# Gate and up projections of an MLP by Strassen's seven block products, in a Mamba, MLP and expert kernel on one Trainium2 core

## The chip, the cores and the metric

The kernel runs on one core of one Trainium2 chip. A core has five engines that run side by side, each through its own list of instructions in order: TensorE (PE) multiplies matrices, VectorE (DVE), ScalarE (ACT) and GpSimd (POOL) work on vectors, SyncE (SP) issues transfers. ACT and POOL issue some transfers too.[...] Matrix products land in PSUM, a memory of eight banks per core, from which DVE and ACT take them. The metric is the device time of one execution in microseconds (us).

## What is computed

All arithmetic is in 32-bit floats. There are 2048 tokens of 512 numbers. The reference, cut to what matters:

```python
x = x + attn_ref(layernorm(x), ...)
x = x + ffn_ref(layernorm(x), ...)

def attn_ref(hidden_states, ...):
    residual = hidden_states
    h = rmsnorm(hidden_states, ln1_w)
    h = residual + mamba2(h, ...)
    residual = h
    h2 = rmsnorm(h, ln2_w)
    mlp = silu(h2 @ gate_w) * (h2 @ up_w) @ down_w
    return residual + mlp

def mamba2(x, ...):
    z, xb, Bc, Cc, dt = split(x @ in_proj_w)
    xBC = silu(causal_depthwise_conv(concat(xb, Bc, Cc)))
    dt = softplus(dt + dt_bias)
    y = ssd_chunked(x_h * dt, dt * A, B_h, C_h) + D * x_h
    return rmsnorm(y * silu(z), norm_w) @ out_proj_w
```

gate_w and up_w are 512x2048, down_w is 2048x512. ffn_ref picks 2 of 8 experts for each token and sums their weighted outputs.

## The kernel before

The code is one function written in a tile language: the program says which tiles exist, how many buffers a kind of tile has, and in which engine an operation runs. A scheduler then puts the instructions of each engine in an order, by the program's order and its own idea of when things are ready. So instructions of different stages come to stand between each other.

Four stages run over the tokens.

- Mamba, in blocks of 256 tokens (`mamba`, L650 on). `prepare` normalizes x and turns it (`hn`, `pt`, `hT`), and computes dt with many small DVE steps (`pdt`, L214 to L236). `project` multiplies by in_proj (`pm`, L300), ACT copies the result out (`pre`, L310), DVE runs the convolution as eight steps a pair (L317 and L319), ACT applies Silu (L323). `gate` makes z (`pz`, L300, Silu L329). `chunk` runs the state-space part for 128 tokens: 16 Exps on ACT (L367), products with dt on DVE (L369), matmuls `psc`, `py`, `pst`. At its end ACT squares y, POOL adds the squares up (`sq`, L427), PE sums them over partitions (`pms`, L430), and PE multiplies y by out_proj (`po`, L437). `pms` is written ahead of `po`.
- MLP, in blocks of 512 tokens (`feed_forward`, `mlp`, `mlp_down`). For each chunk c of 128 of the 2048 hidden columns: `pg` and `pu` are four matmuls each of a 128x128 weight block with 512 columns of h2T; ACT takes Silu of pg (L594), DVE multiplies by pu (L595). For every two chunks, `mlp_down` makes four products `pd` (L603) that DVE adds to the rows (L606). There are 4 blocks x 16 chunks. The first three blocks run in between the Mamba steps, one chunk per step; the fourth runs after Mamba, while expert weights are loaded.
- Routing (`route`), for each block of 512 tokens, in between the next block's chunks.
- Experts (`tiles`), 39 tiles of 128 gathered tokens, after the MLP.

PSUM before: a ring of two banks for transposes and small sums (`ps_tr`), a ring of three for pm, pz, po, pg, pu and pd (`ps_mm`), one tile of two banks for psc, one bank for py. For the last MLP block and the experts there are two banks each of four kinds.

SP issues nearly all loads: x, the weights of in_proj (`wi`, four buffers of 512 KB, loaded three ahead), gate, up and down weights for each chunk (`mg`, `mu`, `md`), the broadcast rows of dt sums (`cum`, `ec`). Each load waits in SP's list until its buffer is free. At the start POOL scales out_proj's weights by norm_w (L457).

The matmuls of 32-bit floats are each two instructions in the trace.

Of the kernel before, what the change touches and what calls it, by code (L numbers as in the profile page):

```python
# [15 lines left out]
P = 128  # L16
T = 2048
D = 512
# [10 lines left out]
DFF = 2048  # L29
FC = 128  # L30
# [18 lines left out]
def mamba_mlp_moe(ctx, tc, x, w_in, w_out, w_gate, w_up, w_down, par, wr, wg, wu, wd, out):  # L49
# [20 lines left out]
    xp = pa_stack.enter_context(tc.tile_pool(name="xp", bufs=6))  # L70
# [8 lines left out]
    params = const.tile([P, NPAR], F32, name="params")  # L79
# [4 lines left out]
    for t in range(NCH):  # L84
        load_x(t)
# [4 lines left out]
    def load_w_in(pair):  # L90

        w = pw.tile([P, NK, 2 * P], F32, name="wi", tag="wi", bufs=4)
        nc.sync.dma_start(out=w, in_=w_in_k[:, :, pair * 2 * P : (pair + 1) * 2 * P])
        return w

    ahead = [load_w_in(pair) for pair in range(3)]
    for t in range(NCH, 2 * NCH):
        load_x(t)
# [12 lines left out]
    late = const.tile([P, P], F32, name="late")  # L111
# [9 lines left out]
    halo = const.tile([P, 12, 3], F32, name="halo")  # L121
# [11 lines left out]
    )  # L133
    a_neg = const.tile([P, NH], F32, name="a_neg")
    nc.scalar.activation(a_neg, params[:, C_AL : C_AL + NH], AF.Exp)
    nc.vector.tensor_scalar_mul(a_neg, a_neg, -1.0)
# [26 lines left out]
    ps_tr = psa_stack.enter_context(tc.tile_pool(name="ps_tr", bufs=2, space=PSUM))  # L163
# [4 lines left out]
    use = {"g": (ps_mm, "mm"), "u": (ps_mm, "mm"), "d": (ps_mm, "mm"), "tr": (ps_tr, "tr")}  # L168
# [5 lines left out]

    def scales(b):
        lo, hi = b * NCH, (b + 1) * NCH
        for t in range(lo, hi):
            stats(wa, res[t], mv[:, t, :])
        rsqrt_eps(rstd[:, lo:hi], mv[:, lo:hi, 1])
        ms = wa.tile([P, NCH], F32, name=f"ms{lo}", tag="ms")  # L180
        nc.vector.tensor_tensor(ms, mv[:, lo:hi, 1], rstd[:, lo:hi], ALU.mult)
        nc.vector.tensor_tensor(ms, ms, rstd[:, lo:hi], ALU.mult)
        rsqrt_eps(rboth[:, lo:hi], ms)
        nc.vector.tensor_tensor(rboth[:, lo:hi], rboth[:, lo:hi], rstd[:, lo:hi], ALU.mult)
# [11 lines left out]
    def prepare(b):  # L196
# [11 lines left out]
        yield hT  # L208


        pdt = ps_tr.tile([P, NCH, NH], F32, name=f"pdt{b}", tag="tr")
# [26 lines left out]
        yield  # L238

# [4 lines left out]
        pc = ps_tr.tile([P, P], F32, name=f"pc{b}", tag="tr")  # L244
# [7 lines left out]
        pn = ps_tr.tile([P, NCH, NH], F32, name=f"pn{b}", tag="tr")  # L252
# [7 lines left out]
        psum = ps_tr.tile([P, 2, NCH, NH], F32, name=f"psum{b}", tag="tr")  # L260
# [33 lines left out]
    def projected(b, pair, pm, hT):  # L294
        w = ahead.pop(0)
        if b < NB - 1 or pair < 7:
            ahead.append(load_w_in((pair + 3) % 10))
        for m in range(2):
            for k in range(NK):
                nc.tensor.matmul(  # L300
                    pm[:, m, :], w[:, k, m * P : (m + 1) * P], hT[:, k, :], start=(k == 0), stop=(k == NK - 1)
                )

    def project(b, pair, hT, xb, cs):
# [8 lines left out]
        for m in range(2):  # L313
# [4 lines left out]
            for k in range(1, 4):  # L318
                nc.vector.scalar_tensor_tensor(  # L319
                    ca, pre[:, m, k : k + TB], cw[:, k : k + 1], ca, ALU.mult, ALU.add  # L320
                )
            dst = xb[:, ct, :] if ct < 4 else cs[(ct - 4) // 4][:, ct % 4, :]
# [8 lines left out]
    def channels(b):  # L331
        xb = wa.tile([P, 4, TB], F32, name=f"xb{b}", tag="xb")
        return xb, [wa.tile([P, 4, TB], F32, name=f"cs{b}_{g}", tag="cs", bufs=4) for g in range(2)]

    state = None
    h2T = [None] * NFB

    def chunk(b, j, dt, ncum, dtdec, cd, cum, ec, xb, cs, zs):
        nonlocal state
# [3 lines left out]
        sdt = sdiag[t % 2]  # L343


        pt = ps_tr.tile([P, 4, P], F32, name=f"ptx{t}", tag="tr")
# [5 lines left out]
        y = wa.tile([P, 8, P], F32, name=f"y{t}", tag="y")  # L352
        for gp in range(2):
# [38 lines left out]
            if gp == 0 and t < NT - 1:  # L392
                pst = ps_tr.tile([P, 2, 4, HD], F32, name=f"pst{t}", tag="tr")
# [3 lines left out]

            for i in range(4):
                at = C_D + 4 * gp + i
                nc.vector.scalar_tensor_tensor(  # L400
                    y[:, 4 * gp + i, :], xb[:, gp, tok], params[:, at : at + 1], py[:, i, :], ALU.mult, ALU.add
                )
            yg = y[:, 4 * gp : 4 * gp + 4, :]
            nc.vector.tensor_tensor(yg, yg, zs[:, 4 * gp : 4 * gp + 4, tok], ALU.mult)

        if t < NT - 1:
            new = wa.tile([P, 2, 4, HD], F32, name=f"state{t}", tag="state")
            flat = new.rearrange("p g i d -> p (g i) d")
            if t:
                nc.gpsimd.tensor_tensor(  # L410
                    flat, state.rearrange("p g i d -> p (g i) d"),
                    bc(cd[:, j].rearrange("p g i -> p (g i)"), 2, HD), ALU.mult,
                )
                nc.vector.tensor_tensor(new, new, pst, ALU.add)
            else:
                nc.vector.tensor_copy(new, pst)
            state = new
# [11 lines left out]
        pms = ps_tr.tile([P, 1], F32, name=f"pms{t}", tag="tr")  # L429
        nc.tensor.matmul(pms, sq[:, 0, :], ones[:, 0:1], start=True, stop=True)  # L430

# [3 lines left out]
        po = ps_mm.tile([P, D], F32, name=f"po{t}", tag="mm")  # L435
        for m in range(8):
            nc.tensor.matmul(po, y[:, m, :], w_o[:, m, :], start=(m == 0), stop=(m == 7))  # L437
# [14 lines left out]
        if off == 0:  # L452
            h2T[fb] = wk.tile([P, NK, FB], F32, name=f"h2T{fb}", tag="h2T")
        transposed(h2, h2T[fb][:, :, off : off + P], params[:, C_L2 : C_L2 + NK])
# [5 lines left out]
    def load_mlp(c):  # L460
        g = pmlp.tile([P, NK, FC], F32, name="mg", tag="mg")
        u = pmlp.tile([P, NK, FC], F32, name="mu", tag="mu")
        d = pmlp.tile([P, D], F32, name="md", tag="md", bufs=4)
        cols = slice(c * FC, (c + 1) * FC)
        nc.sync.dma_start(out=g, in_=w_gate[:, cols].rearrange("(k p) n -> p k n", p=P))
        nc.sync.dma_start(out=u, in_=w_up[:, cols].rearrange("(k p) n -> p k n", p=P))
        nc.sync.dma_start(out=d, in_=w_down[cols, :])
        return g, u, d

    def row(name):  # L470
        if more_rows:
            return more_rows.tile([P, D], F32, name=name, tag="row3", bufs=5)
        return wk.tile([P, D], F32, name=name, tag="row", bufs=5)

    def mid(shape, name):
        return wk.tile([P, *shape], F32, name=name, tag="mid", bufs=5)
# [109 lines left out]
    def mlp(fb, hT, c, w):  # L586
        g, u, d = w
        pg = bank("g", [FB], f"pg{fb}_{c}")
        pu = bank("u", [FB], f"pu{fb}_{c}")
        for wt, ps in ((g, pg), (u, pu)):  # L590
            for k in range(NK):
                nc.tensor.matmul(ps, wt[:, k, :], hT[:, k, :], start=(k == 0), stop=(k == NK - 1))  # L592
        a = wk.tile([P, FB], F32, name=f"a{fb}_{c}", tag="mid", bufs=5)
        nc.scalar.activation(a, pg, AF.Silu)  # L594
        nc.vector.tensor_tensor(a, a, pu, ALU.mult)  # L595
        return a

    def mlp_down(fb, rows, c, held):

        for j in range(NJ):  # L600
            pd = bank("d", [D], f"pd{fb}_{c}_{j}")
            for m, (a, d) in enumerate(held):
                nc.tensor.matmul(  # L603
                    pd, a[:, j * P : (j + 1) * P], d, start=(m == 0), stop=(m == len(held) - 1)
                )
            nc.vector.tensor_tensor(rows[j], rows[j], pd, ALU.add)  # L606

    def feed_forward(fb):

        nonlocal mlp_w, newest  # L610
        if fb == 0:
            mlp_w = load_mlp(0)
        rows = []
        held = []
        for c in range(NFC):
            w = mlp_w
            if fb < NFB - 1 or c < NFC - 1:
                mlp_w = load_mlp((c + 1) % NFC)
# [335 lines left out]
```

## Time and profile before

| | |
|---|---|
| median of 3 runs | 1628.93 us (1628.45 to 1629.21) |
| the profiled execution | 1629.27 us, of which the span in the profile is 1627.2 us |
| granted clock of PE | 0.993 of full speed |
| pd, down products (L603), busy | 225.4 us in 512 instructions |
| pm and pz, in_proj (L300), busy | 182.9 and 115.1 us in 768 and 512 instructions |
| po, out_proj (L437) | 118.4 us in 256 instructions |
| expert products (L817, L838) | 118.2, 117.8 and 107.6 us |
| first chunk's Silu of pg (L594) starts | 222.3 us |
| last one starts | 1276.8 us |

The page of a profile gives busy time by engine, then the span in 40 equal slices, each with a digit for the busy tenths; then the chain of work that ended last; then groups of instructions by line: engine, operation, tile written and tiles read, shape, count, then busy time and the mean of one in ns, then how long the engine stood idle just before them and what ended that. In the timeline each line has a start, a length, an engine, a line and an operation, and in brackets the idle time ahead of it. Busy time of a group leaves out what overlaps with other instructions of the engine, the mean does not.

### The profile page before, as it was taken

Reading aid. Unit: us, or ns where it says so; the run is one execution under the profiler, and the core shown is the slowest. Engines: PE = TensorE matmul, PEld = TensorE weight load, DVE = VectorE, ACT = ScalarE, POOL = GpSimd, SP = SyncE. Lnnn points to the kernel's source line nnn. Section 1 sums busy time; section 2 is a strip of 40 time slices with the busy share of each in tenths; the row PEclk is TensorE's granted clock in tenths of the full one; section 3 lists DMA queues with packets and bytes.
Section 4 is the critical chain, followed back from the end, with each engine's and each line's share of the span. In section 5 each row is a group of like instructions: output and inputs, shape, how many; then the busy total and the mean of one; then the engine's idle time right before and its main releaser. Section 6 shows DMA issues by size and latency. Waiting matters only on the chain.

```text
span 1627.2 us, 16530 instructions
## 1 busy us (share of the span) xinstructions
PE 1581.5 (97%) x5515; PEld 906.4 (56%) x5515; DVE 706.1 (43%) x1835; ACT 600.2 (37%) x1033; POOL 299.8 (18%) x349
## 2 busy tenths in 40 slices
PE   6989899999999999999999999999999999999997
PEld 5656565555555655555565556444444565666653
DVE  5876654544454456445454653233432342222221
ACT  4988784334342634262435333211100121111110
POOL 4332211211021102110211020000010014333321
PEclk9999899999999999999999999999999999999999
DMA  7634333323343633342335321216676124333332
GB/s 243 196 115 137 110 117 117 117 89 109 94 119 99 184 97 116 89 119 89 106 117 163 117 90 50 61 59 215 214 228 185 59 44 86 65 66 66 67 48 33
DMA packets 165202, 182.86 MB, mean 112 GB/s; under 512 B 10432, under 2 KB 125632, under 8 KB 165120
## 3 DMA queue, kind: packets, MB, share of 16 engines
q1 hardware_dynamic: 147456, 145.10, 30.3%
q0 software_dynamic: 8736, 20.45, 7.4%
q10 hardware_dynamic: 8928, 16.26, 2.7%
q8 instruction: 46, 0.75, 0.2%
q14 instruction: 36, 0.29, 0.1%
HBM read 155.04 MB, written 26.74 MB: 112 GB/s over the span
## 4 chain that ended last, share of the span: by engine, by line
PE 90%; ACT 2%; DVE 2%; DMA 2%; issue 2%; POOL 1%; SPq 0%; POOLq 0%; ACTq 0%; DVEq 0%
PE pg L592 13%; PE pu L592 13%; PE pd L603 13%; PE pm L300 9%; PE po L437 6%; PE epd L838 6%; PE epu L817 6%; PE epg L817 6%; PE pz L300 5%; PE pt L190 2%; PE psc L361 2%; PE py L388 2%; PE py L382 2%; PE pdt L214 1%; PE pl L515 1%
## 5 line engine op out<-in xcount | busy, mean ns | idle before, releaser
L592 PE MATMUL pg<-h2T,mg 128*128 128x512 f32 x512 | 231.8, 593 | 0.0
L592 PE MATMUL pu<-h2T,mu 128*128 128x512 f32 x512 | 230.2, 592 | 0.0
L603 PE MATMUL pd<-md,a 128*128 128x512 f32 x512 | 225.4, 592 | 0.0
L300 PE MATMUL pm<-hT,wi 128*128 128x256 f32 x768 | 182.9, 390 | 0.0
L595 DVE TENSOR_TENSOR a<-a,pu 128x512 f32<-128x512 f32 x64 | 44.0, 688 | 285.4 <-PE pu L592 255.9
L603 PEld LDWEIGHTS pd<-md,a 128*128 128x128 f32 x512 | 97.1, 190 | 122.3 <-issue 120.1
L592 PEld LDWEIGHTS pu<-h2T,mu 128*128 128x128 f32 x512 | 97.2, 190 | 122.0 <-issue 118.2
L300 PEld LDWEIGHTS pm<-hT,wi 128*128 128x128 f32 x768 | 145.4, 194 | 33.8 <-issue 12.6
L592 PEld LDWEIGHTS pg<-h2T,mg 128*128 128x128 f32 x512 | 96.1, 190 | 98.6 <-issue 95.5
L606 DVE TENSOR_TENSOR r<-r,pd 128x512 f32<-128x512 f32 x128 | 88.0, 687 | 116.1 <-PE pd L603 113.1
L319 DVE SCALAR_TENSOR_TENSOR ca<-pre,params,ca 128x256 f32<-128x256 f32 x288 | 127.8, 503 | 0.6
L817 PE MATMUL epg<-ew,xgT 128*128 x312 | 118.2, 461 | 0.5 <-issue 0.5
L437 PE MATMUL po<-w_o,y 128*128 128x512 f32 x256 | 118.4, 610 | 0.0
L817 PE MATMUL epu<-ew,xgT 128*128 x312 | 117.8, 459 | 0.0
L300 PE MATMUL pz<-hT,wi 128*128 128x256 f32 x512 | 115.1, 381 | 0.0
L838 PE MATMUL epd<-ew,ehT 128*128 (+1 forms) x234 | 107.6, 594 | 0.5 <-DVE ehT L831 0.5
L300 PEld LDWEIGHTS pz<-hT,wi 128*128 128x128 f32 x512 | 95.5, 190 | 13.5 <-DMA wi<-in_w_in 0.8
L367 ACT ACTIVATE cum<-cum,ncum 128x128 f32<-128x128 f32 x256 | 85.1, 391 | 25.3 <-POOL cum L281 24.8
L594 ACT ACTIVATE a<-pg 128x512 f32<-128x512 f32 x64 | 37.7, 589 | 151.8 <-PE pg L592 148.8
L367 ACT ACT_TABLE_LOAD x65 | 83.4, 1283 | 1.6 <-issue 0.6
L844 POOL DMA_INDIRECT out<-ey,idx x39 | 61.8, 1585 | 94.2 <-DVE ey L843 78.1
L798 POOL DMA_INDIRECT xg<-xnd,idx x39 | 38.3, 981 | 211.7 <-PE pt L190 187.0
(220 smaller groups left out, 1755.8 us busy)
## 6 DMA issues: line engine op xcount, KB each, us to landing
wi<-in_w_in SPq DMA_DIRECT2D x80, 512.0 KB, 3.8
mg<-in_w_gate SPq DMA_DIRECT2D x64, 256.0 KB, 2.8
mu<-in_w_up SPq DMA_DIRECT2D x64, 256.0 KB, 2.8
md<-in_w_down SPq DMA_DIRECT2D x64, 256.0 KB, 2.8
cum<-rowsd SPq DMA_DIRECT2D x32, 512.0 KB, 4.9
ec<-rowsd SPq DMA_DIRECT2D x60, 128.0 KB, 4.2
xnd<-xn ACTq DMA_DIRECT2D x28, 256.0 KB, 4.5
ew<-in_wg SPq DMA_DIRECT2D x8, 704.0 KB, 5.8
```

Of the source, the lines that this page charges most:

```text
L300: nc.tensor.matmul(pm[:, m, :], w[:, k, m * P : (m + 1) * P], hT[:, k, :], start=(k == 0), stop=(k == NK - 1))
L319: nc.vector.scalar_tensor_tensor(ca, pre[:, m, k : k + TB], cw[:, k : k + 1], ca, ALU.mult, ALU.add)
L367: nc.scalar.activation(lt[:, half, i], lt[:, half, i], AF.Exp, bias=ncum[:, j, h : h + 1])
L437: nc.tensor.matmul(po, y[:, m, :], w_o[:, m, :], start=(m == 0), stop=(m == 7))
L592: nc.tensor.matmul(ps, wt[:, k, :], hT[:, k, :], start=(k == 0), stop=(k == NK - 1))
L595: nc.vector.tensor_tensor(a, a, pu, ALU.mult)
L603: nc.tensor.matmul(pd, a[:, j * P : (j + 1) * P], d, start=(m == 0), stop=(m == len(held) - 1))
L606: nc.vector.tensor_tensor(rows[j], rows[j], pd, ALU.add)
L798: nc.gpsimd.indirect_dma_start(out=xg, out_offset=None, in_=src, in_offset=bass.IndirectOffsetOnAxis(ap=idx[:, n : n + 1], axis=0))
L817: nc.tensor.matmul(ps, xT[:, k, :], w[:, lo : lo + EI], start=(k == 0), stop=(k == NK - 1))
L838: nc.tensor.matmul(pd, hT[:n, m, :], w[:n, NG + m * D : NG + (m + 1) * D], start=(m == 0), stop=(m == len(ET) - 1))
L844: nc.gpsimd.indirect_dma_start(out=out, out_offset=bass.IndirectOffsetOnAxis(ap=idx[:, n : n + 1], axis=0), in_=y, in_offset=None, compute ...
```

## The change

The gate and up products of a chunk are seen as one product of two by two blocks: the weights [gate; up] in halves of the 512 inputs, h2T in halves of its inputs and in halves of its 512 tokens. A plain product takes eight block products; Strassen's algorithm, in Winograd's form, takes seven, with sums of weight blocks and of h2T blocks ahead, and sums of products behind. A block product is two matmuls of 128x128 with 256 columns, added up in PSUM.

- The sums of h2T (`sums`) are made once per 512 tokens, two on DVE and two on POOL, of 128x512 each. The sums of weights are made by POOL in the first MLP block (four of 128x256 a chunk), stored to DRAM by ACT, and read from there in the three later blocks.
- Products go to two tiles: `px` (the code's x1) takes five of the seven, the last three added in PSUM onto what is there, and `py` (x2) takes two, the second added onto the first. ACT copies px or py out three times a chunk, DVE adds or multiplies four times, POOL multiplies once, Silu comes in two halves.
- `mlp_down` is spread: two of the four pd for a pair of chunks between the products of each later chunk.
- PSUM: one bank each for px and py, and one ring of three for all that was in the two rings before. The last MLP block still has two banks of each kind.
- The first four x tiles are loaded first; the two norms in a row take one square root in place of two on the way to `hn`; `a_neg` and `rstd` are made later. `pms` is written behind `po`.
- To make room: five x buffers for six, three of wi for four (two ahead), y written into zs, the state updated in place, fewer buffers for rows, gathers two tiles ahead for four.

The diff, cut to its core:

```diff
-    for t in range(NCH):
+    for t in range(2 * NCH):
         load_x(t)
...
-        rsqrt_eps(rstd[:, lo:hi], mv[:, lo:hi, 1])
-        ms = wa.tile([P, NCH], F32, name=f"ms{lo}", tag="ms")
-        nc.vector.tensor_tensor(ms, mv[:, lo:hi, 1], rstd[:, lo:hi], ALU.mult)
-        nc.vector.tensor_tensor(ms, ms, rstd[:, lo:hi], ALU.mult)
-        rsqrt_eps(rboth[:, lo:hi], ms)
-        nc.vector.tensor_tensor(rboth[:, lo:hi], rboth[:, lo:hi], rstd[:, lo:hi], ALU.mult)
+        nc.scalar.activation(rboth[:, lo:hi], mv[:, lo:hi, 1], AF.Sqrt, bias=eps2, scale=1.0 + EPS)
+        nc.vector.reciprocal(rboth[:, lo:hi], rboth[:, lo:hi])
...
-        pms = ps_tr.tile([P, 1], F32, name=f"pms{t}", tag="tr")
-        nc.tensor.matmul(pms, sq[:, 0, :], ones[:, 0:1], start=True, stop=True)
...
         po = ps_mm.tile([P, D], F32, name=f"po{t}", tag="mm")
         for m in range(8):
             nc.tensor.matmul(po, y[:, m, :], w_o[:, m, :], start=(m == 0), stop=(m == 7))
+        pms = ps_mm.tile([P, 1], F32, name=f"pms{t}", tag="mm")
+        nc.tensor.matmul(pms, sq[:, 0, :], ones[:, 0:1], start=True, stop=True)
...
+    def load_late(fb, c, w):
+        v = pmlp.tile([P, 4, KH, FC], F32, name="ms", tag="mg", bufs=3)
+        if fb == 0:
+            nc.sync.dma_start(out=v[:, 3], in_=w_gu[c, :, 1, 1])
+            nc.gpsimd.tensor_tensor(w[:, 2], w[:, 3], v[:, 3], ALU.add)
+            nc.gpsimd.tensor_tensor(v[:, 0], w[:, 2], w[:, 0], ALU.subtract)
+            nc.gpsimd.tensor_tensor(v[:, 1], w[:, 0], w[:, 3], ALU.subtract)
+            nc.gpsimd.tensor_tensor(v[:, 2], w[:, 1], v[:, 0], ALU.subtract)
+            nc.scalar.dma_start(out=early_d[c], in_=w[:, 0:3])
+            nc.scalar.dma_start(out=late_d[c], in_=v)
+        else:
+            nc.sync.dma_start(out=v, in_=late_d[c])
+        return v
...
+        def product(ps, w, m, first=True):
+            for k in range(KH):
+                nc.tensor.matmul(
+                    ps, w[:, k], m[:, k], start=(first and k == 0), stop=(k == KH - 1), skip_group_check=True
+                )
...
+            product(x1, early[:, 1], b21)
+            nc.scalar.copy(a[:, 0], x1)
+            product(x2, early[:, 2], t1)
+            nc.scalar.copy(up, x2)
+            if more:
+                mlp_w = coming, load_late(*to, coming)
+            product(x1, early[:, 0], b11)
+            nc.vector.tensor_tensor(a[:, 0], a[:, 0], x1, ALU.add)
+            nc.scalar.activation(a[:, 0], a[:, 0], AF.Silu)
+            product(x2, late_[:, 2], b22, False)
+            product(x1, late_[:, 0], t2, False)
+            nc.scalar.copy(part, x1)
+            if pair:
+                mlp_down(fb, rows, 2 * (c % 2), pair)
+            product(x1, late_[:, 1], t3, False)
+            nc.vector.tensor_tensor(a[:, 1], part, x2, ALU.add)
+            nc.vector.tensor_tensor(up, up, x1, ALU.add)
+            nc.scalar.activation(a[:, 1], a[:, 1], AF.Silu)
+            if pair:
+                mlp_down(fb, rows, 2 * (c % 2) + 1, pair)
+            product(x1, late_[:, 3], t4, False)
+            nc.vector.tensor_tensor(a[:, 0], a[:, 0], x1, ALU.mult)
+            nc.gpsimd.tensor_tensor(a[:, 1], a[:, 1], up, ALU.mult)
...
-    AHEAD = 4
+    AHEAD = 2
```

In the text, the early weights are the three blocks of `load_early`, the late ones the four of `load_late`.

## The prediction

> **What bounds the kernel now.** I read the page first, then the waits, then the timeline where the changed steps run.
>
> ```profile
> span 1627.2 us, 16530 instructions
> PE 1581.5 (97%) x5515; PEld 906.4 (56%) x5515; DVE 706.1 (43%) x1835; ACT 600.2 (37%) x1033; POOL 299.8 (18%) x349
> PE   6989899999999999999999999999999999999997
> ACT  4988784334342634262435333211100121111110
> PE 90%; ACT 2%; DVE 2%; DMA 2%; issue 2%; POOL 1%; SPq 0%; POOLq 0%; ACTq 0%; DVEq 0%
> L592 PE MATMUL pg<-h2T,mg 128*128 128x512 f32 x512 | 231.8, 593 | 0.0
> L592 PE MATMUL pu<-h2T,mu 128*128 128x512 f32 x512 | 230.2, 592 | 0.0
> L319 DVE SCALAR_TENSOR_TENSOR ca<-pre,params,ca 128x256 f32<-128x256 f32 x288 | 127.8, 503 | 0.6
> L367 ACT ACT_TABLE_LOAD x65 | 83.4, 1283 | 1.6 <-issue 0.6
> ```
>
> TensorE (PE) bounds it: the chain of what ended last is 90% PE, and from 300 us on its slices are full. Gate and up together are 462 us of its time. Only at the start is another engine as full: ScalarE (ACT) has 7 to 9 tenths in slices 2 to 5. So removed matmuls pay in full, and a wait that makes PE stand idle costs in full. PE's own waits are few:
>
> ```profile
> PE pt L190 <- DVE hn L203: 15.7, 3, 14.2
> PE pms L430 <- POOL sq L427: 12.6, 4, 6.5
> ```
>
> A mean of 593 ns holds the tail of a pipelined matmul; what counts is the distance between starts:
>
> ```profile
> 614.68 3.62 PE L300 MATMUL pm<-hT,wi 128*128 128x256 f32 x16
> 618.14 3.60 PE L592 MATMUL pg<-h2T,mg 128*128 128x512 f32 x8
> 621.57 3.60 PE L592 MATMUL pu<-h2T,mu 128*128 128x512 f32 x8
> ```
>
> (618.14-614.68)/16 = 0.2163 us for 256 columns, (621.57-618.14)/8 = 0.4288 us for 512. One f32 matmul of the code is two instructions (512 pg for 256 in the code). What ACT and VectorE (DVE) do after a projection, and what POOL does at the start:
>
> ```profile
> 19.35 13.42 POOL L457 TENSOR_SCALAR w_o<-w_o,params 128x512 f32<-128x512 f32 x8 [14.02 <-DMA w_o<-in_w_out]
> 25.18 0.59 ACT L310 COPY pre<-pm 128x512 f32<-128x512 f32 x1 [4.37 <-PE pm L300]
> 752.49 0.59 ACT L310 COPY pre<-pm 128x512 f32<-128x512 f32 x1 [5.02 <-PE pm L300]
> 753.17 0.61 DVE L317 TENSOR_SCALAR ca<-pre,params 128x256 f32<-128x256 f32 x2 [2.30 <-issue]
> 753.70 2.46 DVE L319 SCALAR_TENSOR_TENSOR ca<-pre,params,ca 128x256 f32<-128x256 f32 x6
> ```
>
> The matmuls pm ended at 752.29, the copy began 0.20 later, the eight convolution steps ended at 756.16: 3.9 us after PE.
>
> **What the skill says.** "TensorE: Matmul & The Clock Gate", Back-to-back issue gap, gives 262 cycles for 256 columns and 518 for 512, a ratio of 0.506; the trace has 0.2163/0.4288 = 0.504, so half-width products lose almost nothing. Weight loads, 28 for 16, still hide: 190 ns each below 216. "ScalarE: Activation LUTs", What ACT_TABLE_LOAD costs, prices a switch at 1283 ns and a drain of 1380 ns more; the trace agrees on 1283, and shows no drain behind it (a load at 700.59, the next ACTIVATE at 701.88). "PSUM — Partial Sum Buffer", Engine vs sequencer instructions, calls the ACT, DVE and POOL queues strict FIFO. The trace agrees: at 85.04 ACT issued the store of resd, which needs POOL's sum, and its next work waited 0.95 us for POOL.
>
> **The change, part by part.** Its compiled order of instructions per engine can be read without running it, and I lean on that order, with durations from the trace.
>
> *Products.* Per chunk c of 128 hidden columns and 512 tokens: 16 instructions of 512 go, 7 products x 2 blocks x 2 = 28 of 256 come. 16 x 0.4288 = 6.86 us, 28 x 0.2163 = 6.06 us. For 64 chunks: 439.1 - 387.6 = **-51.5 us**, all on PE's path.
>
> *Waits inside a chunk.* px (x1) takes five of the seven products, one bank in the first three quarters of the MLP. A product is 4 x 0.2163 = 0.87 us. Reuse after ACT's copy: 0.20 to start, about 0.37 for 128x256 (interpolated from 583 ns for 128x512 and 262 ns for 96x128), about 0.1 back: 0.67, covered by the py product. Reuse after DVE's sum: 0.20+0.42 (422 ns, lists<-pls) + 0.1 = 0.72, covered also. That is with free engines. In the merged stretches DVE does the eight convolution steps before L671's sum: that ends 3.9+0.4 = 4.3 us after pm; PE needs it after four products and one pd, 4 x 0.87+0.86 = 4.3. The order is made to fit so, without slack. What I find late is ACT: between the two copies of some chunks stands an Exp with a table load (1.28+0.39), and loads rise from 197 to 224 in the order. Walking the six chunks of a block that stand beside projections, by hand, most chunks wait 0 to 0.3 us, one (c=13, behind four to eight Exps and the convolution they hold up) about 2.4, and one with routing on DVE about 0.8. That is some 4 to 5 us per 16 chunks; for three feeds **+14**. Bounds: 0, if ACT runs ahead, and 48 x 1.5 = 72, if every chunk meets a burst. The new ACT work itself (three copies, two Silu halves for one Silu, some +1.6 us a chunk) fits: ACT was 35 to 48% busy in the windows of 100 us from 300 to 800.
>
> *Weight sums of the first feed.* Four POOL sums of 128x256 a chunk (723 ns each by the sq row) behind a load that can start only when the chunk's third product has freed the buffer: 2.6 us, load 2.8 (256 KB row), three sums after it 2.2, then ACT, which issues both stores in its own queue ahead of Silu and the copy of part: 7.6+0.3+0.5+0.4 = 8.8 us. PE reaches the next use at about 8.8. Any late transfer is paid: I take 0.75 us x 16 = **+12**, bounds 0 and 32. Traffic doubles for these weights (917 KB read for 512 KB in three feeds, 14.7 MB written), but mean DMA share is near 0.37[...].
>
> *Start.* x is loaded first and one square root is saved, so the first transposes come at about 9 us for 14.18. But pm now stands behind the whole dt chain (at best 5 us of small DVE steps after pdt), and ACT's third DMA, the store of the first weight sums, stands ahead of every copy pre. POOL makes these sums behind the 13.4 us of w_o. Up to w_o 4.1 MB are queued for 4.6: at the same rate it lands at about 17.3, +13.4+2 x 0.72 = 32.2 before ACT goes on, and the second store holds it to 33.9. So pre_0 ends near 34.5 for 25.77. The ring of three is full behind it, and the convolutions follow with ACT's alternating Exp and Silu tables. ACT is nearly full up to 160 us, so most stays: **+9**. Bounds -5 (all absorbed) and +12.
>
> *pms moved.* It waits 12.6 us now; moved behind po it is covered only by what is left of po: at 117.27 two instructions, at 198.17 four, so 0.9 and 1.7, and the small waits of 1.19 and 0.25 wholly: **-4**. Bounds 0 and -12.6.
>
> *The rest at nothing.* The last feed has two banks of each kind and an idle ACT and DVE; its gain is in the sum above. The ring of three, wi with three buffers and x with five cost nothing by the compiled order, which places their users; pg and pu no longer take slots of the ring. In the expert tiles a gather needs 1.0+3.7 us and now gets a buffer two tiles ahead, 16 us (8.1 a tile). State in place and y in zs only shorten lives of buffers.
>
> Sum: -51.5+14+12+9-4 = -20.5. On the profiled span 1627.2 that is 1606.7; 2.1 us lie around the span (1629.27), and the median is 0.3 lower: **1608 us**.
>
> **Rivals.** *All hidden*: waits, weights and start cost nothing, pms gains 4: 1628.9-55.5 = 1573. For it: the compiled order moves pd and py between px products where they would wait. Against: ACT's table loads and POOL's start. *Slower*: the one-bank px chain becomes the bound while mamba runs beside it. Its place is the reuse of px and py after ACT's copies in feeds 0 to 2; its price is the wait per chunk over 48 chunks. With start and pms as above, it decides from (51.5-9+4)/48 = 0.97 us on; with 1.5 us it is 1628.9-46.5+72 = 1654. For it: ACT holds 23 to 28 table loads in a mamba block, and before a Silu had pu and pd, 3 to 5 us, as cover. Against: my walk finds most chunks near zero. *Half products not half*: if weights do not hide and the spacing is the group mean of pm, 182.9/768 = 0.238, 1792 x 0.238 = 426.8; the gain is 12, and with the other costs it ends at 1648.
>
> **How the numbers follow.** My forecast 0.57, all hidden 0.13, slower chain 0.25, spacing 0.05. The forecast's own range is 1590 to 1632: a tenth of it lies on the slower side or at no change. About 0.2% (3 us) is what can be told from no change. Faster: 0.51 and 0.13 and 0.02 of the others, 0.66; same 0.05; slower 0.29. The range reaches to 1575 below, near all hidden, and to 1648 above.
>
> **What would show it.** PE's matmuls of the products at 0.216 us apart; PE's waits with px or py on ACT's copies summing to 20 to 30 us up to 1000 us, and none in the last feed; ACT standing on POOL near 32 us; the waits of pms at 8 us or so. Waits of px over 47 us, or starts more than 0.23 apart, prove me wrong on the slow side; a start no later than before, with px waits under 10, on the other.

## The result, and the profile after

The changed kernel takes 1641.47 us (median of 11, 1633.21 to 1646.97), the kernel before 1628.45 beside it (11, 1626.83 to 1629.94): 1.008 times as long, 95% interval 1.0064 to 1.0096. The forecast was 1608. The profiled execution took 1641.24 us, span 1639.5. From its page (engines with busy share and count; the slices of PE and ACT):

```profile
span 1639.5 us, 19005 instructions
PE 1560.9 (95%) x6283; PEld 1056.3 (64%) x6283; DVE 780.5 (48%) x2011; ACT 714.9 (44%) x1316; POOL 401.5 (24%) x486
...
PE   4998989999999999999999999999999989999997
...
ACT  2987857444653565455636454523211211111110
```

PE is busy only 20.6 us less than before, though 52 us of its work went. The products themselves are as forecast. From the timeline of PE:

```profile
1180.89 1.03 PE L644 MATMUL px<-h2T,mg 128*128 128x256 f32 x4
1181.76 1.03 PE L644 MATMUL py<-ts,mg 128*128 128x256 f32 x4
1182.62 1.03 PE L644 MATMUL px<-h2T,mg 128*128 128x256 f32 x4
1183.48 1.03 PE L644 MATMUL py<-h2T,ms 128*128 128x256 f32 x4
```

(1183.48-1180.89)/12 = 0.216 us per instruction. Most of what was lost is waiting. The waits of PE over the whole span (total us, times, longest):

```profile
PE pt L186 <- DVE hn L199: 10.2, 2, 9.9
PE pt L186 <- DVE h L448: 9.1, 4, 4.0
PE px L644 <- DVE a L671: 7.6, 12, 1.2
PE pc L246 <- DVE dA L243: 6.3, 1, 6.3
PE pls L606 <- DVE v L604: 5.3, 4, 1.4
PE pm L301 <- DMA wi<-in_w_in: 4.8, 1, 4.8
PE px L644 <- ACT a L665: 4.6, 6, 1.3
PE pms L432 <- POOL sq L425: 4.4, 2, 2.3
PE pl L542 <- ACT xT L188: 3.2, 4, 1.0
```

New are the px waits, pc and pm at the start, and pls and pl, which belong to the last routing among the expert tiles. These lines are a floor: a stall that is shorter than the tail of the matmul before it shows as busy. The Trainium skill, "Perfetto Trace Analysis", Identifying the Most-Contended Engine, says that matmul busy time is no good measure of how close a kernel is to the limit, and the trace agrees: busy 97% before and 95% after, with 52 us less to do. So I took the distances between starts. For each shape, the distance that a fifth of its instructions stay under counts as work; what a distance has beyond that counts as rest, waits and slower matmuls alike. The stages are marked by po, the out_proj product of a tile of 128 tokens (an MLP block follows four tiles), and by epg, the first product of an expert tile. By stage, before and after, in us:

| stage | length | PE's work | rest | of the rest, ahead of px and py of the MLP |
|---|---|---|---|---|
| to the first po (first matmul at 14.2, 9.9) | 73.2, 86.4 | 44.2, 44.8 | 14.6, 31.5 | 0 |
| to po of tile 4 | 190.8, 187.4 | 142.5, 136.1 | 48.5, 51.3 | 2.6 |
| first MLP block, to po of tile 8 | 305.9, 317.6 | 282.0, 274.7 | 23.9, 43.0 | 16.1 |
| second, to po of tile 12 | 312.6, 306.9 | 287.9, 275.0 | 24.6, 31.9 | 8.3 |
| third, to the end of the last po | 214.1, 202.0 | 196.6, 181.3 | 17.4, 20.8 | 6.1 |
| fourth, to the first epg | 191.8, 187.4 | 189.4, 178.8 | 2.0, 8.1 | 6.7 |
| experts, to the last matmul | 328.8, 341.9 | 302.5, 302.6 | 26.3, 39.3 | 0 |

Work fell by 51.8, rest rose by 68.6, and the first matmul came 4.3 earlier: +12.5, for 12.3 between the spans. (The expectations below count by fixed times, so 38.8 for the 39.8 us of the last column, 29.4 for 33.1 ahead of the fourth block and 13.1 for 16.1 in the first.) The largest surprise is the last row: 13 us in a stage that runs no Strassen product.

Part of the rest is the clock. In the profile the granted clock of PE is either full or half. Leaving out the last matmuls of the span, it is half for 17.1 us in two stretches before, and for 34.1 us in six after, four of these ahead of po of tile 4. One of the six runs from 1138.3 to 1141.7 us; from the timeline of PE:

```profile
1139.73 1.91 PE L644 MATMUL px<-ts,ms 128*128 128x256 f32 x4
1141.43 1.17 PE L629 MATMUL pd<-md,a 128*128 128x512 f32 x2
```

(1141.43-1139.73)/4 = 0.425 us per instruction, for 0.216 at full clock. Counting for each distance in these stretches at most its work over again, matmuls at half speed make about 5.9 us of the rest before and 13.8 after: 8 of the 68.6. Ahead of each stretch, before and after, PE had 1.7 to 4.3 us of rest in 6.8 us, so it looks like a consequence of the waits; no run tried it apart. Traces are single executions, too: in five whose first MLP block is coded alike its px and py waits lie between 13.3 and 16.1 us, and in nine with the same fourth block between 4.5 and 9.6.

### The profile page after: what moved, and what is told of

The parts are those of the page before. It is cut to its first block, busy times and chain, and to the rows that moved or that the text cites. A ratio compares the mean times of both kernels' runs of the same rounds, so it can differ in the third digit from the quotient of the medians.

```text
span 1639.5 us, 19005 instructions
## 1 busy us (share of the span) xinstructions
PE 1560.9 (95%) x6283; PEld 1056.3 (64%) x6283; DVE 780.5 (48%) x2011; ACT 714.9 (44%) x1316; POOL 401.5 (24%) x486
## 5 line engine op out<-in xcount | busy, mean ns | idle before, releaser
L629 PE MATMUL pd<-md,a 128*128 128x512 f32 x512 | 244.2, 592 | 0.0
L686 POOL TENSOR_TENSOR a<-a,up 128x256 f32<-128x256 f32 x64 | 46.8, 732 | 396.0 <-DVE up L680 281.2
L644 PE MATMUL px<-ts,ms 128*128 128x256 f32 x512 | 134.9, 386 | 7.8 <-DVE a L671 7.6
L644 PE MATMUL px<-h2T,mg 128*128 128x256 f32 x512 | 135.0, 385 | 4.7 <-ACT a L665 4.6
L320 DVE SCALAR_TENSOR_TENSOR ca<-pre,params,ca 128x256 f32<-128x256 f32 x288 | 136.4, 538 | 0.1
L644 PEld LDWEIGHTS px<-ts,ms 128*128 128x128 f32 x512 | 91.5, 191 | 65.0 <-DVE a L671 21.5
L644 PEld LDWEIGHTS px<-h2T,mg 128*128 128x128 f32 x512 | 94.9, 190 | 29.4 <-ACT a L665 8.8
L430 PE MATMUL po<-w_o,zs 128*128 128x512 f32 x256 | 113.8, 593 | 0.0
L430 PEld LDWEIGHTS po<-w_o,zs 128*128 128x128 f32 x256 | 48.5, 190 | 52.6 <-issue 51.4
L671 DVE TENSOR_TENSOR a<-a,px 128x256 f32<-128x256 f32 x64 | 26.6, 415 | 114.2 <-PE px L644 108.8
```

Of the source, the lines that this page charges most:

```text
L320: nc.vector.scalar_tensor_tensor(ca, pre[:, m, k : k + TB], cw[:, k : k + 1], ca, ALU.mult, ALU.add)
L629: nc.tensor.matmul(pd, a[:, j * P : (j + 1) * P], d, start=(m == 0), stop=(m == 1))
L644: nc.tensor.matmul(ps, w[:, k], m[:, k], start=(first and k == 0), stop=(k == KH - 1), skip_group_check=True)
L671: nc.vector.tensor_tensor(a[:, 0], a[:, 0], x1, ALU.add)
L686: nc.gpsimd.tensor_tensor(a[:, 1], a[:, 1], up, ALU.mult)
```

## The experiments

Each was timed beside the kernel before (1627.4 to 1628.1 us in the four batches). "Ratio" is to that kernel, with its 95% interval.

### The last stage

The routing of the last 512 tokens runs among the expert tiles, and both take their intermediates (xn, xT, v, eh and others) from `mid`, now three buffers for five. From the waits of ACT between 1285 and 1400 us, changed kernel:

```profile
ACT xT L188 <- DMA xnd<-xn: 10.3, 2, 5.7
```

and from its timeline:

```profile
1307.71 0.33 ACTq L535 DMA_DIRECT2D xnd<-xn  x1
...
1308.12 0.60 PE L186 MATMUL pt<-ident,xn 128*128 128x128 f32 x4
...
1309.84 0.59 ACT L188 COPY xT<-pt 128x512 f32<-128x512 f32 x1 [5.71 <-DMA xnd<-xn]
```

PE's transposes were written by 1308.7, but the copy out of PSUM began at 1309.84: it needed a buffer that a store of xn still read. The kernel before has no such wait there. Run e_tail (turn[0] is set once the last chunk of the MLP has been issued, when a's buffers fall free):

```diff
     def mid(shape, name):
+        if turn[0] is not None:
+            turn[0] += 1
+            if turn[0] % 2:
+                return wk.tile([P, *shape], F32, name=name, tag="a", bufs=4)
         return wk.tile([P, *shape], F32, name=name, tag="mid", bufs=3)
...
         if more_rows:
+            if int(name[2:]) % 3:
+                return pmlp.tile([P, D], F32, name=name, tag="md", bufs=4)
...
-    AHEAD = 2
+    AHEAD = 4
```

> The changed kernel with more buffers in the expert stage only: the intermediates of the last routing and of the expert tiles take turns between their ring of three and the four buffers of a, which nothing uses any more, gathered rows lie in six buffers for two (the four of md beside the two), and AHEAD is 4 again. Theory (the 13 us that the expert stage lost come from rings that are too short: xT and xn wait for a buffer that a store of xn or a tile's eh holds): the stage from the first epg to the last goes from 336.8 us back to about 324, the waits pls<-v (5.3 us) and pl<-xT (2.6 us) go, and the time falls by 10 to 13 us, to 1628 to 1632. Rival (the stage is longer because the last routing shares PE, DVE and PSUM with the tiles from a later start, whatever its buffers): within 2 us of 1641.5. Second rival (half and half, the pls part being the chain of small DVE steps): -5 us.

1625.03 us, ratio 0.9983 (0.9974 to 0.9992): 16.4 less than the changed kernel, more than the theory's 10 to 13. From the first epg to the last 322.3 us for 336.7 (before: 323.6). In that stage pls and pl are gone from PE's waits. e_tailmid has only the first of the three hunks:

> The changed kernel with only the first half of the edit for the expert stage: the intermediates of the last routing and of the tiles take turns between their three buffers and the four of a; gathered rows keep two buffers and AHEAD stays 2. Theory (the ring of intermediates, in which xT waits for the stores of xn, is what cost the 14.5 us): the last stage takes 322 to 326 us and the time is 1625 to 1629. Rival (the gathers, of which only two could be ahead, cost most of it): the last stage stays above 332 us and the time above 1635.

1625.78 us, ratio 0.9991 (0.9978 to 1.0003), stage 321.9. So it was the intermediates; the fewer rows and shorter gathers cost nothing that these runs can tell.

The converse is the kernel before with a ring of three. A first try, b_cut, handed three tiles out by turns by hand:

```diff
     def mid(shape, name):
+        if three:
+            turn[0] += 1
+            flat = three[turn[0] % 3][:, :size]
...
```

> The kernel before the change, with one edit: in the last routing and the expert tiles the intermediates share three buffers, as in the changed kernel, for five. Rows and AHEAD stay at 5 and 4. Theory (the ring of three costs the last stage 14 us by itself, without any of Strassen's products): the stage from the first epg to the last goes from 323.6 us to 333 to 338, and the time from 1627.9 to 1638 to 1643. Rival (it cost that much only beside the changed kernel's other edits): the stage stays under 327 us and the time within 4 us of 1628.

It took 1667.34 us, ratio 1.0248, and decides nothing: the last routing and the tiles behind it compute other values, most likely because some tiles were overwritten before their last reader, and PE's work in the stage is 324.6 us for 302.5. b_cut2 leaves the turns to the pool; beside the edit shown, it makes the room with x at five buffers for six, the rows of the last stage at four for five and AHEAD at 3 for 4:

```diff
-        return wk.tile([P, *shape], F32, name=name, tag="mid", bufs=5)
+        return wk.tile([P, *shape], F32, name=name, tag="mid", bufs=3)
...
-        a = wk.tile([P, FB], F32, name=f"a{fb}_{c}", tag="mid", bufs=5)
+        a = wk.tile([P, FB], F32, name=f"a{fb}_{c}", tag="a", bufs=3)
```

> The kernel before the change with a ring of three for the intermediates: mid has three buffers, a has three of its own, and to make room x has five buffers for six, and the last stage's rows four for five with AHEAD 3. The computation is the same. Theory (the ring of three costs the last stage 14 us by itself, without any of Strassen's products): the stage from the first epg to the last goes from 323.6 us to 333 to 338. Rival (it cost that much only beside the changed kernel's other edits): it stays under 327 us. The time itself also holds what the other two cuts do to the stages ahead, so the theory has it 9 to 16 us above 1627.4 and the rival within 5 us of it.

1644.15 us, ratio 1.0107 (1.0085 to 1.0128). The stage takes 338.9 us for 323.6, and it starts at 1288.7, where the kernel before has it at 1288.5. Its waits of PE from 1285 to 1400 us show the changed kernel's own line again, to the tenth; first the kernel before, then b_cut2:

```profile
PE pls L579 <- DVE v L577: 0.2, 1, 0.2
...
PE pls L579 <- DVE v L577: 5.3, 4, 1.4
```

ACT's wait for the store of xn is back as well, with 8.6 us. So the ring of three costs 13 to 15 us in these traces, with or without Strassen. b_cut2 alone can't tell it from the rows and AHEAD, but e_tailmid, which leaves both short, has no such loss. Some of the loss is half clock: none before, about 1.3 us in the changed kernel's last stage and 4.1 in b_cut2's, which leaves 11 to 12 us of waits in each.

### The products' waits, and the first block's sums

From the waits of ACT between 222 and 600 us, changed kernel: ACT stands at a store until POOL has made the sums, and its next work bears the wait.

```profile
ACT a L672 <- POOL ms L485: 21.2, 7, 4.9
```

e_raw leaves out the sums of weights and their stores, so that the MLP's values are others:

```diff
-        if fb == 0:
-            nc.sync.dma_start(out=w[:, 0:2], in_=w_gu[c, :, 0])
-            nc.sync.dma_start(out=w[:, 3], in_=w_gu[c, :, 1, 0])
-        else:
-            nc.sync.dma_start(out=w[:, 0:3], in_=early_d[c])
+        raw = w_gu[c].rearrange("p a b k n -> p (a b) k n")
+        nc.sync.dma_start(out=w[:, 0:3], in_=raw[:, 0:3])
...
+        nc.sync.dma_start(out=v, in_=w_gu[c].rearrange("p a b k n -> p (a b) k n"))
```

> The changed kernel without the weight sums of the first feed and their stores: every feed reads seven blocks of the given weights as they lie, with as many transfers and bytes as feeds 1 to 3 have now. The MLP's values are not the reference's. Theory (the first feed pays for its sums and for the two stores that ACT issues): the px and py waits of feed 0 fall from 13.1 us to the 7 to 9 us of feeds 1 and 2, ACT's wait at the start goes too, and the time falls by 4 to 6 us for the first and up to 9 us for the second: 1627 to 1637. Rival (these waits come from the reuse of the one bank of px and not from the sums): feed 0 keeps over 11 us of px and py waits, and the time falls only by what the start gives, at most as much as in the run that moves the first stores.

1627.1 us, ratio 1.0 (0.9988 to 1.0013): 14.4 less. The first block takes 306.1 us for 317.6, its px and py waits fall from 16.1 to 8.4; po of tile 4 comes at 266.8 for 273.9. Other values choose other experts, so its last stage (340.4 from epg to epg, 3.7 longer) isn't compared; the first epg comes 17.4 us earlier (1270.3 for 1287.7), so the 14.4 may understate what the sums and stores cost.

The next runs stand on e_tail (1625.0). e_store keeps the sums and moves the stores:

```diff
-            nc.scalar.dma_start(out=early_d[c], in_=w[:, 0:3])
-            nc.scalar.dma_start(out=late_d[c], in_=v)
+            nc.gpsimd.dma_start(out=early_d[c], in_=w[:, 0:3])
+            nc.gpsimd.dma_start(out=late_d[c], in_=v)
```

> On top of the version with more buffers in the expert stage (1625.0 us): all 32 stores of the first feed's weight sums are issued by POOL behind its sums, none by ACT. The sums stay. Theory (of the 14.4 us that leaving sums and stores out gained, most is ACT standing at a store until POOL has made the sums, 21.2 us of its waits between 222 and 1015 us): the time falls by 6 to 12 us, to 1613 to 1619, and feed 0's px and py waits from 15 to under 10 us. Rival (the late pieces themselves are what the products wait for, or POOL becomes late with Mamba's work by issuing): within 2 us of 1625.0, or above it.

1619.43 us, ratio 0.9943 (0.993 to 0.9956): 5.6 less, just short of the theory's 6. The first block takes 310.9 us for 316.6, its px and py waits are 11.2 for 15.1 (theory: under 10). So about 6 us, of the 14 to 17, were ACT's standing at stores; the rest stays with the sums.

Does a px product wait because its bank is filled again too soon? e_order, on the changed kernel, puts more products between writing and reuse and uses two half banks:

```diff
-            product(x1, early[:, 1], b21)
-            nc.scalar.copy(a[:, 0], x1)
+            product(x1, early[:, 0], b11)
+            product(x0, early[:, 1], b21, False)
+            nc.scalar.copy(a[:, 0], x0)
...
-            product(x2, late_[:, 2], b22, False)
-            product(x1, late_[:, 0], t2, False)
+            product(x1, late_[:, 0], t2, False)
             nc.scalar.copy(part, x1)
...
+            product(x2, late_[:, 2], b22, False)
```

> The changed kernel with the products of a chunk put in another order, and with px's two half banks used in turn: 1 (gate's second product) goes into the other half, so that no product waits for its copy; the product that adds to py and the one that adds to px come after the first pair of down products; and a chunk starts in the half that the one before it has left. The computation is the same. Theory (the 38.8 us of px and py waits, 29.4 of them in feeds 0 to 2, come from a bank that is written again 0.86 us after it was filled, while ACT or DVE still has to read it): px and py waits fall under 15 us and the time by 15 to 25 us, to 1617 to 1627. Rival (they come from ACT and DVE being late with work for Mamba, whatever the distance, or from weights that are late): waits stay over 30 us and the time falls by less than 5 us.

1641.22 us, ratio 1.0069 (1.005 to 1.0088): no gain. The waits were 19.3, 8.8 and 5.4 us in the first three blocks (16.1, 8.3, 6.1 before the edit); only in the fourth were they less, 3.7 for 6.7, and that is hardly outside the 4.5 to 9.6 of other traces. (The profiled execution was the slowest of six, 1648.68 us, so its waits may be high; the median says the same.) The longest grew. From the waits of PE, 222 to 1015 us, of e_order:

```profile
PE px L645 <- DVE a L673: 13.9, 13, 2.9
```

The sum that empties px comes late, however far off its deadline. So the distance between filling and refilling isn't what costs the time. Is that for ACT's copy ahead of it? e_dve gives two of the copies to DVE:

```diff
-            nc.scalar.copy(a[:, 0], x1)
+            nc.vector.tensor_copy(a[:, 0], x1)
...
-            nc.scalar.copy(part, x1)
+            nc.vector.tensor_copy(part, x1)
```

> On top of the version with more buffers in the expert stage (1625.0 us): DVE makes two of the three copies out of px in a chunk (the one that a product of px waits for and part), instead of ACT. Theory (products of px wait because ACT is late with the copy, with Mamba's exponentials and their table loads ahead of it in its queue): the px and py waits of feeds 0 to 2, 27 to 28 us here, fall by half, and the time by 8 to 14 us. Rival (DVE, with the convolutions in its queue, is as late as ACT, and the add that follows the copy was already DVE's): waits within 5 us of what they were and the time within 3 us of 1625.0; above it if DVE gets later for Mamba.

1634.9 us, ratio 1.0039 (1.0026 to 1.0052): 9.9 more than e_tail. Waits fell in the first block (15.1 to 12.4) and rose in the second (7.4 to 11.9), which is 8.7 us longer. From the same view of e_dve (L673 and L683 are the moved copies):

```profile
PE px L652 <- DVE a L673: 6.2, 6, 1.3
...
PE px L652 <- DVE part L683: 3.5, 3, 1.5
```

The third block's rose too, from 5.0 to 7.0. Both engines are late now and then, with Mamba's work in the same queues, and moving these copies to DVE made it worse.

### The start

From the timeline of ACT, changed kernel:

```profile
32.12 0.33 ACTq L486 DMA_DIRECT2D early<-mg  x1
32.50 0.20 ACT L264 ACTIVATE dtdec<-psum 128x32 f32<-128x32 f32 x1 [9.61 <-POOL mg L482]
...
33.73 0.33 ACTq L487 DMA_DIRECT2D late<-ms  x1
34.10 0.59 ACT L311 COPY pre<-pm 128x512 f32<-128x512 f32 x1 [1.15 <-POOL pre L312]
```

The prediction had ACT held to 32.2 and 33.9 us, and the end of pre_0 at 34.5; it is 34.69. But is this what costs the 9 us? e_start moves these two stores alone:

```diff
-            nc.scalar.dma_start(out=early_d[c], in_=w[:, 0:3])
-            nc.scalar.dma_start(out=late_d[c], in_=v)
+            q = nc.scalar if c else nc.gpsimd
+            q.dma_start(out=early_d[c], in_=w[:, 0:3])
+            q.dma_start(out=late_d[c], in_=v)
```

> The changed kernel with the two stores of the very first weight sums (feed 0, chunk 0) issued by POOL, behind its own sums, instead of by ACT; the other 15 pairs of stores stay on ACT. Theory (ACT stood 9.6 us on these stores and everything before 222 us came later by it): pre_0 starts near 24.5 us for 34.1, the first po comes 4 to 9 us before its 86.4, and the time falls by 4 to 9 us, to 1632.5 to 1637.5. Rival (POOL's scaling of w_o holds pre_1's halo to 33.6 us in any case, and the third wi comes late, so that ACT's wait was hidden): pre_0 comes early, the first po within 1.5 us of 86.4, and the time within 2 us of 1641.5.

1641.21 us, ratio 1.0079 (1.0066 to 1.0092): no gain. The timeline of ACT in e_start shows why:

```profile
28.93 0.59 ACT L311 COPY pre<-pm 128x512 f32<-128x512 f32 x1 [4.40 <-PE pm L301]
37.46 0.69 ACT L369 ACTIVATE cum<-cum,ncum 128x128 f32<-128x128 f32 x2 [7.95 <-POOL cum L282]
```

pre_0 is 5.2 us earlier, and the next instruction waits 7.95 us for POOL's mask of cum, behind w_o and the sums in POOL's queue. The first po came at 86.0 us for 86.4. The four runs that follow, each named with its base, tried the rest. e_wo (on e_tail):

```diff
-    for m in range(8):
-        nc.gpsimd.tensor_scalar_mul(w_o[:, m, :], w_o[:, m, :], params[:, C_NW + m : C_NW + m + 1])
...
     near = [spread(0, j, ready[-1]) for j in range(NCH)]
+    for m in range(8):
+        nc.vector.tensor_scalar_mul(w_o[:, m, :], w_o[:, m, :], params[:, C_NW + m : C_NW + m + 1])
```

> On top of the version with more buffers in the expert stage (1625.0 us): DVE scales w_o by the norm's weights instead of POOL, 8 instructions among the steps of dt, so that POOL makes the first sums, the halos and the masks of cum as soon as they are there. Theory (the start is late because pre, the cum exponentials behind it on ACT and the convolutions wait for POOL's 12.4 us of w_o, of which the store was only one case): pre_1 ends near 32 to 35 us for 41.2, the first po starts 5 to 10 us before its 86.4, and the time falls by 4 to 9 us. Rival (ACT's own work up to 222 us sets the pace, whatever the start): the first po within 2 us of 86.4 or the gain gone by 274 us, and the time within 2 us of 1625.0.

1624.46 us, ratio 0.9979 (0.9969 to 0.9989), 0.6 less; first po at 86.8. DVE now stood 2.5 us at w_o, until 17.96 us, with dt's steps behind, so pc's wait grew from 6.3 to 10.9. e_first (on e_store):

```diff
-    ready = finish(prepare(0))
-    near = [spread(0, j, ready[-1]) for j in range(NCH)]
+    coming0 = prepare(0)
+    hT0 = next(coming0)
     xc = channels(0)
+    project(0, 0, hT0, *xc)
+    next(coming0)
+    project(0, 1, hT0, *xc)
+    next(coming0)
+    project(0, 2, hT0, *xc)
+    ready = finish(coming0)
```

> On top of the version with more buffers in the expert stage and with the stores of the first feed on POOL (1619.4 us): the first three input projections stand ahead of the steps of dt in the program, one before each step, as they do in every later block. Theory (the start lost 13 us because transposes, dt's small products and projections now share one ring of three, which is taken in the order of the program, so that pm_0 waits for pn, which waits for the dt chain): pm_0 starts near 12 to 14 us for 23.7, pre_0 ends near 20 us for 29.1, the first po starts at 72 to 80 us for 85.2, and the time falls by 4 to 12 us, to 1607 to 1615. Rival (POOL's scaling of w_o holds the halos and the masks of cum until 31 us anyway, or dt's steps come so much later that they set the pace): the first po within 3 us of 85 and the time within 2 us of 1619.4.

1620.38 us, ratio 0.9965 (0.9952 to 0.9977), the same as e_store within the intervals. pre_0 ended at 19.4 and pre_1 at 25.7 us, but pre_2 at 44.2 and the first po at 88.6. e_first3 is e_first and e_wo together:

> As the run before, and DVE scales w_o instead of POOL. With the projections first, DVE stands at w_o (18 us) with dt's steps and the first convolution behind it, but POOL is free for halos and sums. Theory (with the ring's order mended, POOL is what is late next): the first po 2 to 5 us before that of the run before, and the time 2 to 4 us less. Rival (DVE's stand at w_o costs as much as it gives, as it did when it was tried alone): within 2 us of the run before.

1616.78 us, ratio 0.9935 (0.9921 to 0.995): 3.6 less than e_first and the lowest median of all, though its interval overlaps those of e_store and e_first5; the first po at 86.3, 2.3 earlier. e_first5 (on e_first):

```diff
+    nw = pw.tile([P, 8], F32, name="nw")
+    nc.vector.scalar_tensor_tensor(
+        nw, xc[1][0][:, 3, 0:8], 0.0, params[:, C_NW : C_NW + 8], ALU.mult, ALU.add
+    )
...
-        nc.gpsimd.tensor_scalar_mul(w_o[:, m, :], w_o[:, m, :], params[:, C_NW + m : C_NW + m + 1])
+        nc.gpsimd.tensor_scalar_mul(w_o[:, m, :], w_o[:, m, :], nw[:, m : m + 1])
```

> On top of the version with more buffers in the expert stage, the first feed's stores on POOL and the projections ahead of dt's steps (1620.4 us): POOL's scaling of w_o is held back until a convolution of the fourth projection is there, by reading the weights of the norm through an instruction of DVE that waits for it. Theory (the start is late because w_o stands ahead of the halos and masks on POOL, now that the ring's order is mended): pre_1's convolution no longer waits 10.7 us, pre_2 ends near 33 us for 44.2, the first po starts at 72 to 80 us for 88.6, and the time falls by 5 to 12 us, to 1608 to 1615. Rival (ACT's tables, silus and exponentials set the pace up to the first po): the first po stays above 83 us and the time within 3 us of 1620.4.

1619.33 us, ratio 0.9944 (0.9932 to 0.9955); first po at 84.7: the rival. From 40 us to the first po ACT is busy 31.3 of 33.2 us before, 44.8 of 46.4 after, 39.3 of 44.7 in e_first5. It did 16.2 us of work before 40 us in the kernel before, 8.5 in the changed one, 12.0 in e_first5. And the new order puts 71 of its instructions ahead of the first po (table loads left out), where the kernel before had 55; the 16 more are the Exps of a second chunk. So ACT's order may be the cause, but it is argued from these counts: no run changed it alone, and with 64 ahead of it, in the three runs with projections first, the first po came no earlier than 84.7.

Two other candidates stand in PE's waits up to 90 us. The one for wi, which has a buffer less, is 4.8 us in the changed kernel; it is 0.7 in e_store and gone in e_wo and e_first5, with the first po at 84.7 to 86.8 all the same, so it isn't the cause. The one at pc, a small product of dt that now shares the ring of three PSUM banks with the projections, is 6.3 us in the changed kernel and 6.7 to 13.0 in the other runs of this section and e_store, for 1.5 before. No run gave these products a ring of their own again. The cause of the late start stays open.

## Why the prediction was wrong

The step that failed is the last of the sum, *the rest at nothing*: it gave the last stage no cost, and the runs show 13 to 16 us there. The other terms first.

*Products*, -51.5: right. PE's work fell by 51.8 us.

*Waits inside a chunk*, +14, and *Weight sums of the first feed*, +12: 33.1 us of px and py waits before the fourth block, for 26 together. The first term is under-sized: the second and third blocks have 14.4 us and, with the sums left out, the first has 8.4, so some 23. That the wait is for a late engine and not for the bank as such fits e_order. But the late engine was to be ACT, with its copies; from 222 to 1015 us PE's waits name DVE's sum of L671 with 7.6 us and ACT's copies with 4.5. The second term holds in size: without sums and stores the first block is 11.5 us shorter. But only 7.7 of these were px and py waits, and 5.6 us of the time went with the stores. (The traffic for these weights does not double: 384 and 512 KB a chunk are 896 for 512. Nothing rests on it.)

*Start*, +9: the size came out right, the reason did not, so the match is luck. po of tile 4 came 9.8 us later, but ACT's stores, named as the cause, only stood in front of a wait nearly as long: removing them gave nothing. Of the 9.8 about 4.9 are matmuls at half clock.

*pms moved*, -4: its waits went from 12.6 to 4.4 us, where it expected about 8. No stage shows the gain apart, and no run tried it alone.

*The rest at nothing* failed in two of its claims, and they decide the sign of the change. For the last stage the step asked of the expert tiles only whether a gather gets its buffer in time. That was right (e_tailmid). It didn't ask the same of `mid`, which went from five buffers to three in the same diff and is shared with the last routing, where stores and PSUM copies hold it: 13 us in the trace, 16.4 by the medians of e_tail, which without it is faster than before. And "the last feed has two banks of each kind and an idle ACT and DVE": px and py waited 6.7 us in it. PE's waits from 1015 to 1290 us name late weights (1.7 us), the copy up (1.5) and the copy a (1.0), and about 1.2 us is half clock; no run tried these apart. That the PSUM ring of three costs nothing, which the step also said, is open because of the wait at pc.

With the last stage's term the forecast would have been 1621 to 1624, and faster than before still; with the fourth block's 6.7 and the 9 that the chunks' waits were short, 1637 to 1640; with pms's 4 given up as well, 1641 to 1644. That sum is made after the fact. The half clock, which no term had, lies inside these waits and does not come on top. No rival had the last stage: the slower one put its price on the px chain, at 0.97 us for each of 48 chunks or more, where about 0.7 was paid (33.1/48). So its sign, px waits over 47 us, never showed: most of the loss lay where no sign had been set.

Most of what was lost at the end and in the stores can be had back: e_first3 computes the same as both kernels in 0.9935 of the time before.

## What to carry to other kernels

When a diff pays for one stage with buffers of another, cost the other stage too: list every tile that takes turns in the shortened ring, and for each what ends its life, stores included. Find that stage on a timeline even if no line of its arithmetic changed. And when a wait is found exactly where it was forecast, take it away before calling it the cause: e_start removed the wait that had been forecast, and the next one, nearly as long, stood behind it.

## What was not expected of the hardware

Steps of DVE beside large instructions of POOL took longer. In the changed kernel a convolution step of 128x256 on DVE takes 476 ns (median of 227 with no POOL instruction beside it), 1301 ns beside a mask of cum (9 of them), and 712 beside the weight sums of L484 (16), though 475 beside those of L482 (6). From the timeline of DVE:

```profile
56.08 1.54 DVE L320 SCALAR_TENSOR_TENSOR ca<-pre,params,ca 128x256 f32<-128x256 f32 x1
```

and of POOL:

```profile
56.07 1.27 POOL L358 TENSOR_TENSOR ec<-ec,cs 128x512 f32<-128x512 f32 x1 [1.67 <-ACT cs L326]
```

The step ended 0.28 us after POOL's product had; in its usual 0.48 us it would have ended 0.78 us before. The Trainium skill, "SBUF — State Buffer", Who interferes with whom, says that a DVE instruction with two SBUF inputs contends with a GpSimd instruction that reads SBUF; the trace agrees (pre and ca are both there). The first block's sums are such instructions, 64 of them: part of what they cost may be this, which no run tried apart.

The changed kernel's executions spread over 14 us, those of the kernel before over 3 (11 runs each), and the granted clock goes along: 0.990 in the fastest of the changed kernel and 0.984 in the slowest; 0.991 and 0.983 in the fastest and slowest of e_raw's 22 (1618.44 and 1638.06 us). By an estimate from these figures, 0.006 of 1640 us is 10 us of clock, if PE had work throughout. In all traces of this case the clock is full or half, and ahead of the end of the span a half stretch lasts 3.41, 6.83, 10.24 or 13.65 us. Whether longer waits bring the half clock, or something else brings both, no run here says.
